# Attention of layer 0: scores in runs of nine over seven PSUM tiles of one bank, an exponential per bank, row sums of eight key blocks by DMA

## The chip, the core and the metric

The kernel runs on one core of a Trainium2 chip. TensorE (PE) multiplies, ScalarE (ACT) takes exponentials and copies, VectorE (DVE) adds and normalises, GpSimd (POOL) and SyncE (SP) issue DMAs, which all run on the core's 16 DMA engines. The metric is the device time of one execution in microseconds (us), the median over several executions. A profile is one execution recorded by the hardware profiler; its span can differ a little from the median.

## The reference, cut to what matters

Two images x of 256 channels and 64 x 64 pixels go through two layers. The change is in layer 0 alone, an attention over all 4096 pixels with eight heads of 32 channels:

```python
x = x + _L0_conv_ref(_gn(x), L0_conv_qkv_w, L0_conv_qkv_b, 8)

# _L0_conv_ref(x, qkv_w, qkv_b, num_heads), b = 2, c = 256, n = 4096
qkv = jnp.einsum('bchw,oc->bohw', x, qkv_w) + qkv_b[None, :, None, None]
qkv = qkv.reshape(b, 3, num_heads, head_dim, n)
q, k, v = (qkv[:, 0], qkv[:, 1], qkv[:, 2])
scale = 1.0 / math.sqrt(head_dim)
attn_logits = jnp.einsum('bhci,bhcj->bhij', q, k) * scale
attn_weights = jax.nn.softmax(attn_logits, axis=-1)
out = jnp.einsum('bhij,bhcj->bhci', attn_weights, v)
```

`_gn` normalises over groups of eight channels. Layer 1 is a block of convolutions and small local attentions. It comes after layer 0 of each image and is the same in both kernels.

## The kernel before

The two images (b = 0, 1) are worked through one after the other: statistics and projections, then `attention0`, then layer 1. The projections leave queries and keys in memory as two halves of 32-bit numbers whose sum is the exact value, so that a score is one matmul of fp32r operands with 128 rows (32 channels times four combinations of halves).

**Groups, blocks, units.** An image has 16 groups g: head g // 2 with one half of the 4096 queries, 2048 of them as four columns of T = 512. The keys come in NJ = 32 blocks j of 128. One unit is the score of one key block with one query column, a 128 x 512 matmul into one PSUM bank (L505), so a group has 128 units and an image 2048. ACT takes the exponential of a unit from PSUM (L511) and writes it to SBUF. Then two things are done with it:

- TensorE multiplies it with the values, `quarters` (L521). The four units of a block go to four partition quarters of the group's accumulator `av`, with 32 columns of weights each. A block counts as two steps of 256 columns each ("half blocks" below; each is four matmuls, which the trace shows as eight records), and blocks 0 and 31 are one step of 512 columns.
- its sum over the keys is prepared, `add_rows`: for most blocks DVE adds the unit to the tiles `e` (L550, L558), and for the blocks listed in SUMMED the DMA engines add it to the four parts of `acc` (`add_in_memory`, L566 for the first, a copy, and L568 for the accumulating ones). POOL issues these DMAs. They wait for the exponential and for the addition before them in the same rows. At the next group's start DVE adds `acc` to `e` (L748). Then TensorE sums over the partitions with a matrix of ones (`sum_rows`), ACT copies the product (L598), and some small DMAs and DVE instructions divide the group's result by it (`finish`).

**Places.** Exponentials live in a ring of RING = 28 places of 512 columns each, 17 in the tile `es` and 11 at the end of the tile `v`. In the profile their name is `es` or `v` accordingly. `places` holds the place of each unit, `n_places` counts places given out. A place is written again 28 places later, after the value product, the DVE addition or the DMA that reads it.

**PSUM.** Eight banks: `sa` of three, `sb` of two, `sc` of two, and `av` of one. `scores(spare)` fills all three tiles, seven units, with one exponential for each tile (or two where the ring wraps). When a statistic or a row sum needs a bank (`spare`), `sa` gets two units only and its third bank is lent out.

**The order.** It is written by hand, in a block under `manual_schedule`, for PE, ACT and DVE; the queues of POOL and SP follow their waits in program order. A loop alternates a run of scores with a stretch of value products. How many products go between two runs is worked out from `ready` (blocks whose scores stood before the latest run), `share` (an even spread of the steps, less two) and `must` (blocks whose places the next runs will write again). `wanted` is a queue of uses of a lent bank; one is done after two steps of a round, or at its end. A round ends at a group's end, so that the copy of `av` (L762) can go ahead before the next group's first product. `fetch_head` (at block 4 of an even group: keys and values of the next head) and `fetch_queries` (at a group's end, for the group after the next) issue SP's loads, which wait for free buffers.

The last group of an image is finished in another way: its last three blocks are summed by TensorE straight from the exponentials, in a bank lent at block NJ - 3.

Of the kernel before, what the change touches and what calls it, by code (L numbers as in the profile page):

```python
# [9 lines left out]
F32 = mybir.dt.float32  # L10
I32 = mybir.dt.int32
F32R = mybir.dt.float32r
AF = mybir.ActivationFunctionType
# [4 lines left out]
P = 128  # L18
B, C, H, W = 2, 256, 64, 64
N = H * W  # L20
T = 512
# [4 lines left out]
NH0 = C // HD0  # L26
# [14 lines left out]
def direct_layers(ctx: ExitStack, tc: tile.TileContext, a: dict, out: bass.AP, bad: bass.AP):  # L41
# [3 lines left out]
    nc = tc.nc  # L45
# [11 lines left out]
    psum = {}  # L57
# [307 lines left out]
    SC0 = 1.0 / math.sqrt(HD0)  # L365
# [8 lines left out]
    NJ = N // P  # L374
# [76 lines left out]

    RING, RING_A = 28, 17

    SUMMED = (3, 7, 11, 15, 18, 22, 26)

    def summed(g):

        return SUMMED if g else SUMMED[1:]

# [4 lines left out]
    def attention0(b, xts, held):  # L464
# [10 lines left out]
        n_units = NH0 * 2 * NJ * 4  # L475
# [4 lines left out]
        places = []  # L480
        n_places = 0

        def at_places(first, n):

            while n > 0:
                at = first % RING
                m = min(n, (RING_A if at < RING_A else RING) - at)
                yield m, es[:, at : at + m, :] if at < RING_A else held["es"][:, at - RING_A : at - RING_A + m, :]
                first, n = first + m, n - m

        def scores(spare):

            nonlocal n_places
            bank = None
            for tag, size in (("sa", 3), ("sb", 2), ("sc", 2)):
                first = len(places)
                n = min(size - (spare and size == 3), n_units - first)
                if n <= 0:
                    break
                sc = psum["sc"].tile([P, size, T], F32, tag=tag, name=f"{tag}_{b}_{first}")  # L500
                if spare and size == 3:
                    bank = sc[:, size - 1, :]
                for i in range(n):
                    g, (j, u) = (first + i) // (4 * NJ), divmod((first + i) % (4 * NJ), 4)
                    nc.tensor.matmul(  # L505
                        sc[:, i, :], held["k", g // 2][:, j * P : (j + 1) * P], held["q", g, u // 2][:, u % 2, :],
                        start=True, stop=True,
                    )
                i = 0
                for m, dst in at_places(n_places, n):  # L510
                    nc.scalar.activation(dst, sc[:, i : i + m, :], AF.Exp, scale=SC0)  # L511
                    i += m
                places.extend(range(n_places, n_places + n))
                n_places += size
            return bank

        def quarters(dst, lhs, rhs, start, stop, part=None):

# [17 lines left out]
        def add_rows(g, j):  # L536
            if j == 0:
                sums[g] = psum["sc"].tile([P, T], F32, tag="av", name=f"av_{b}_{g}")
                added[g] = [w4([P, 2, T], f"e_{b}_{g}_{w}") for w in range(2)]
                return  # L540
            for w in range(2):
                dst = added[g][w]
                if j in summed(g):
                    if w == 0:
                        add_in_memory(g, j)
                    continue
                if j == 1:
                    first = two_units(g, 0, w), two_units(g, 1, w)
                    if len(first[0]) == len(first[1]) == 1:
                        nc.vector.tensor_add(dst, first[0][0][1], first[1][0][1])  # L550
                    else:
                        for s in range(2):
                            nc.vector.tensor_add(dst[:, s, :], unit(g, 0, 2 * w + s), unit(g, 1, 2 * w + s))
                    continue
                for s, src in two_units(g, j, w):
                    if g == last and j in SUMMED_LAST:
                        continue
                    nc.vector.tensor_add(dst[:, s, :], dst[:, s, :], src)  # L558
# [11 lines left out]
        def work_of(g, j):  # L570


            if (g, j) < (last, NJ - 3):
                add_rows(g, j)
            for part in (None,) if j in (0, NJ - 1) else range(2):
                if part == 1:
                    yield
                quarters(
                    sums[g], held["v"][:, (g // 2) % 2, j, :], lambda u: unit(g, j, u), j == 0, j == NJ - 1, part
                )  # L580

        def sum_rows(g, rows):
            if g == last:
                for part in range(2):
                    for j in SUMMED_LAST:
                        quarters(rows, ones, lambda u: unit(g, j, u), j == SUMMED_LAST[0], False, part)
                    quarters(rows, ones, lambda u: acc[u], False, False, part)
                    quarters(rows, ones, lambda u: added[g][u // 2][:, u % 2, :], False, True, part)
                return
            quarters(rows, ones, lambda u: added[g][u // 2][:, u % 2, :], True, True)  # L590
# [140 lines left out]
        def steps():  # L731

            for done in range(NH0 * 2 * NJ):
                g, j = divmod(done, NJ)
                if (g, j) == (last, NJ - 3):
                    assert len(places) == n_units
                    held["rows"] = psum["sc"].tile([P, 3, T], F32, tag="sa", name=f"rows_{b}")[:, 2, :]
                    for i in (NJ - 3, NJ - 2, NJ - 1):
                        add_rows(g, i)
                    sum_rows(g, held["rows"])  # L740
                for _ in work_of(g, j):
                    yield done
                if g and j == 0:

                    for w in range(2):
                        dst = added[g - 1][w]
                        for s in range(2) if w == 0 else (slice(0, 2),):
                            nc.vector.tensor_add(dst[:, s, :], dst[:, s, :], acc[s] if w == 0 else pair)  # L748
                    waiting.clear()
                if g and j == 1:  # L750
                    wanted.append(late[0].send)
                if g and j in (9, 17):
                    next(late[0])
                for what in also.get((g, j), ()):
                    what()
                if j == 4 and g % 2 == 0 and g // 2 + 1 < NH0:
                    fetch_head(b, g // 2 + 1, held)
                if j == NJ - 1:
                    waiting.append(g)
                    avs = w4([P, 2, T], f"avs_{b}_{g}")  # L760
                    if g < last:
                        nc.scalar.copy(avs[:, 0, :], sums[g])  # L762
                    copied[g] = avs
                    late[:] = [finish(g)]
                    next(late[0])
                    if g + 2 < NH0 * 2:
                        fetch_queries(b, g + 2, held)
                yield done + 1

        E = mybir.EngineType  # L770
        with tc.manual_schedule(engines={E.PE, E.Activation, E.DVE}):

            per_group = 2 * NJ - 2
            work, begun, taken = steps(), 0, 0
            scores(False)
            final = False
            while not final:
                have = len(places)  # L780
                use = wanted.pop(0) if wanted else None
                bank = scores(use is not None)
                final = have == n_units
                ready = have // 4
                share = have * per_group // (4 * NJ) - 2

                must = sum(place < n_places + 7 - RING for place in places[: 4 * ready : 4])
                if must % NJ == 1:
                    must += 1
                assert must <= ready  # L790
                here = 0
                while begun < ready and (taken < share or begun < must or final or use is not None):
                    if use is not None and here == 2:
                        use(bank)
                        use = None
                        continue
                    here += 1
                    group = begun // NJ
                    begun = next(work)
                    taken += 1  # L800
                    if begun // NJ > group and begun >= must and not final and use is None:
                        break
                if use is not None:
                    use(bank)
            assert next(work, None) is None
            return *finish_last(last), st
# [585 lines left out]
    for b in range(B):  # L1392
        xts = x_first if b == 0 else ahead["xts"]
        w0 = w0_first if b == 0 else ahead["w0"]
        with tc.tile_pool(name=f"ps0_{b}", bufs=8, space=PSUM) as psum["ps"]:
# [7 lines left out]
            held = project0(b, xn, w0)  # L1403
# [571 lines left out]
```

## Time and profile before

| | us |
|---|---|
| median of 3 executions | 3120.94 (3116.66 to 3121.48) |
| span of the profiled execution | 3116.4 |
| attention of image 0 (118 to 1161 us of the span) | 1043 |
| attention of image 1 (1666 to 2709 us) | 1043 |
| ACT L511, exponentials of three banks (es and v) | 810 in 556 |
| ACT L511, exponentials of two banks | 1249 in 1214 |
| DVE L558, additions of 1024 columns | 1553 in 1332 |
| DVE L558, additions of 512 columns | 179 in 264 |

The span is the time from the first to the last instruction of the profiled execution. The four last rows add up the page's groups by shape. Busy times of different engines lie beside one another and don't add up to the span. A matmul's record lasts longer than the time to the next one's start[...]: distances from start to start tell what a matmul costs. The same holds for ACT, in smaller measure.

### The profile page before, as it was taken

The page shows a single profiled execution, that of the slowest core. Times are in us where ns is not written, and L with a number is a line of the kernel's source. Part 1 is how long each engine was busy: PE and PEld are TensorE (multiplying, and loading weights), DVE is VectorE, ACT ScalarE, POOL GpSimd, SP SyncE. Part 2 cuts the span into 40 slices and gives each one's busy share as a digit, 9 for nine tenths or more (in the row PEclk, how much of TensorE's full clock was granted, in tenths as well). Part 3 has the DMA queues.
Part 4 walks back from the last instruction along what each step waited for, and adds up shares of the span by engine and source line. Part 5 has one row for each costly group of instructions (what it writes and reads, how often), then busy time and mean ns, then how long its engine had stood idle before and what let it go on. Part 6 is the DMA issues. An engine that isn't in the chain of part 4 may idle for free. (4 is left out here: it accounts for less than half of the span.)

```text
span 3116.4 us, 62659 instructions
## 1 busy us (share of the span) xinstructions
PE 3031.2 (97%) x25129; PEld 1830.6 (59%) x25129; DVE 2467.0 (79%) x3126; ACT 2313.6 (74%) x2436; POOL 836.7 (27%) x923
## 2 busy tenths in 40 slices
PE   6999999999999999999989999999999999999998
PEld 4555555555555556677755555555555555476765
DVE  4599989999899999856556998989989999834543
ACT  2699999999999984622237999999999999734333
POOL 2022222222222231055301222222222222305440
PEclk9999999999999999999999999999999999999999
DMA  7969679797897761230159687796888975700000
GB/s 241 270 132 185 143 150 172 154 178 150 164 181 154 145 133 33 75 134 29 41 193 268 128 176 151 156 176 138 177 162 164 181 153 123 170 4 4 21 14 22
DMA packets 243787, 424.41 MB, mean 136 GB/s; under 512 B 99112, under 2 KB 109916, under 8 KB 241308
## 3 DMA queue, kind: packets, MB, share of 16 engines
q0 software_dynamic: 94992, 238.36, 39.8%
q1 hardware_dynamic: 147580, 181.68, 21.6%
q8 instruction: 199, 3.26, 0.4%
q14 instruction: 104, 0.85, 0.1%
q10 hardware_dynamic: 912, 0.27, 0.0%
HBM read 119.03 MB, written 68.39 MB: 60 GB/s over the span
## 5 line engine op out<-in xcount | busy, mean ns | idle before, releaser
L558 DVE TENSOR_TENSOR e<-e,es 128x1024 f32<-128x1024 f32 (+1 forms) x956 | 1038.6, 1142 | 79.6 <-ACT es L511 77.9
L521 PE MATMUL av<-es,v 128*32 128x256 f32 (+1 forms) x9644 | 746.7, 390 | 0.0
L558 DVE TENSOR_TENSOR e<-e,v 128x1024 f32<-128x1024 f32 (+1 forms) x640 | 675.2, 1107 | 47.7 <-ACT v L511 46.6
L511 ACT ACTIVATE es<-sa 128x1536 f32<-128x1536 f32 (+1 forms) x444 | 635.7, 1432 | 93.1 <-PE sa L505 54.9
L505 PE MATMUL sa<-q,k 128*128 128x512 f32 x1736 | 561.4, 430 | 9.2 <-ACT avs L598 3.5
L521 PE MATMUL av<-v 128*32 128x256 f32 (+1 forms) x6228 | 506.5, 389 | 0.0
L521 PEld LDWEIGHTS av<-es,v 128*32 128x32 f32 x9644 | 316.1, 109 | 299.4 <-issue 160.6
L505 PEld LDWEIGHTS sa<-q,k 128*128 128x128 f32 x1736 | 280.0, 188 | 291.8 <-issue 135.4
L505 PE MATMUL sc<-q,k 128*128 128x512 f32 x1180 | 371.4, 396 | 1.7 <-ACT es L511 0.7
L505 PE MATMUL sb<-q,k 128*128 128x512 f32 x1180 | 371.0, 395 | 1.1 <-ACT es L511 1.1
L521 PEld LDWEIGHTS av<-v 128*32 128x32 f32 x6228 | 216.5, 109 | 178.6 <-issue 81.2
L511 ACT ACTIVATE es<-sc 128x1024 f32<-128x1024 f32 x296 | 306.9, 1037 | 0.0
L511 ACT ACTIVATE v<-sc 128x1024 f32<-128x1024 f32 x294 | 304.9, 1037 | 0.1
L511 ACT ACTIVATE es<-sb 128x1024 f32<-128x1024 f32 x296 | 302.0, 1020 | 3.8 <-DMA acc<-es 3.8
L511 ACT ACTIVATE v<-sb 128x1024 f32<-128x1024 f32 x294 | 300.0, 1020 | 0.0
L505 PEld LDWEIGHTS sb<-q,k 128*128 128x128 f32 x1180 | 221.2, 188 | 55.4 <-ACT es L511 2.9
L505 PEld LDWEIGHTS sc<-q,k 128*128 128x128 f32 x1180 | 210.5, 188 | 71.8 <-ACT es L511 12.1
L511 ACT ACTIVATE v<-sa 128x1536 f32<-128x1536 f32 (+1 forms) x146 | 209.2, 1433 | 35.6 <-PE sa L505 17.0
L948 PE MATMUL mm<-v,wf 128*128 128x256 f32 x1024 | 227.6, 380 | 1.5 <-DVE z L957 1.5
L568 POOL DMA_DIRECT2D es<-es x116 | 98.9, 853 | 475.6 <-ACT es L511 424.3
L948 PEld LDWEIGHTS mm<-v,wf 128*128 128x128 f32 x1024 | 193.3, 190 | 36.8 <-issue 9.9
L938 POOL TENSOR_TENSOR v<-col 128x512 f32<-128x512 f32 x128 | 165.1, 1316 | 179.2 <-ACT rk_sr L1089 39.2
(262 smaller groups left out, 3179.0 us busy)
## 6 DMA issues: line engine op xcount, KB each, us to landing
acc<-es POOLq DMA_DIRECT2D x128, 512.0 KB, 6.2
acc<-v POOLq DMA_DIRECT2D x84, 512.0 KB, 6.4
es<-es POOLq DMA_DIRECT2D x136, 256.0 KB, 4.5
v<-es POOLq DMA_DIRECT2D x132, 256.0 KB, 5.1
k<-wk_halves SPq DMA_DIRECT2D x64, 512.0 KB
q<-wq_halves SPq DMA_DIRECT2D x256, 128.0 KB
v<-v POOLq DMA_DIRECT2D x90, 256.0 KB, 5.4
es<-v POOLq DMA_DIRECT2D x86, 256.0 KB, 3.9
```

Of the source, the lines that this page charges most:

```text
L505: nc.tensor.matmul(sc[:, i, :], held["k", g // 2][:, j * P : (j + 1) * P], held["q", g, u // 2][:, u % 2, :], start=True, stop=True,)
L511: nc.scalar.activation(dst, sc[:, i : i + m, :], AF.Exp, scale=SC0)
L521: nc.tensor.matmul(dst[HD0 * u : HD0 * u + HD0, n], lhs, rhs(u)[:, n], start=start, stop=stop)
L558: nc.vector.tensor_add(dst[:, s, :], dst[:, s, :], src)
L568: nc.gpsimd.dma_start(out=dst, in_=src, accum_op=ALU.add)
L938: (nc.gpsimd.tensor_add if plus else nc.gpsimd.tensor_sub)(dst, rows(one), rows(two))
L948: nc.tensor.matmul(mm[:, m, r, :], wf[:, k, 4 * r + q, m * P : (m + 1) * P], v[r // 2][:, r % 2, k, :], start=k == 0, stop=k == KC - 1,)
```

## The change

The three PSUM tiles become seven tiles of one bank, `s0` to `s6`, which `next_bank` gives out in turn together with a place. `scores` issues PHASE = 9 units, each with its own exponential. A lent bank is the next one in turn. SUMMED has eight blocks instead of seven, four or three apart in turn. The loop counts differently: it issues a run first and treats all but the last seven scores as `ready` (`behind`), `must` looks ten places ahead (`reach`), the last two steps of a group are done without regard to `share`, and the three last blocks of the image wait until all scores are issued.

```diff
--- before.py
+++ after.py
@@ -451,7 +451,7 @@

     RING, RING_A = 28, 17

-    SUMMED = (3, 7, 11, 15, 18, 22, 26)
+    SUMMED = (3, 6, 10, 13, 17, 20, 24, 27)

     def summed(g):

@@ -488,31 +488,27 @@
                 yield m, es[:, at : at + m, :] if at < RING_A else held["es"][:, at - RING_A : at - RING_A + m, :]
                 first, n = first + m, n - m

-        def scores(spare):
+        BANKS, PHASE = 7, 9
+
+        def next_bank():

             nonlocal n_places
-            bank = None
-            for tag, size in (("sa", 3), ("sb", 2), ("sc", 2)):
-                first = len(places)
-                n = min(size - (spare and size == 3), n_units - first)
-                if n <= 0:
-                    break
-                sc = psum["sc"].tile([P, size, T], F32, tag=tag, name=f"{tag}_{b}_{first}")
-                if spare and size == 3:
-                    bank = sc[:, size - 1, :]
-                for i in range(n):
-                    g, (j, u) = (first + i) // (4 * NJ), divmod((first + i) % (4 * NJ), 4)
-                    nc.tensor.matmul(
-                        sc[:, i, :], held["k", g // 2][:, j * P : (j + 1) * P], held["q", g, u // 2][:, u % 2, :],
-                        start=True, stop=True,
-                    )
-                i = 0
-                for m, dst in at_places(n_places, n):
-                    nc.scalar.activation(dst, sc[:, i : i + m, :], AF.Exp, scale=SC0)
-                    i += m
-                places.extend(range(n_places, n_places + n))
-                n_places += size
-            return bank
+            at = n_places
+            n_places += 1
+            return at, psum["sc"].tile([P, T], F32, tag=f"s{at % BANKS}", name=f"s_{b}_{at}")
+
+        def scores():
+
+            for unit in range(len(places), min(len(places) + PHASE, n_units)):
+                g, (j, u) = unit // (4 * NJ), divmod(unit % (4 * NJ), 4)
+                at, sc = next_bank()
+                nc.tensor.matmul(
+                    sc, held["k", g // 2][:, j * P : (j + 1) * P], held["q", g, u // 2][:, u % 2, :],
+                    start=True, stop=True,
+                )
+                ((_, dst),) = at_places(at, 1)
+                nc.scalar.activation(dst[:, 0, :], sc, AF.Exp, scale=SC0)
+                places.append(at)

         def quarters(dst, lhs, rhs, start, stop, part=None):

@@ -734,7 +730,7 @@
                 g, j = divmod(done, NJ)
                 if (g, j) == (last, NJ - 3):
                     assert len(places) == n_units
-                    held["rows"] = psum["sc"].tile([P, 3, T], F32, tag="sa", name=f"rows_{b}")[:, 2, :]
+                    held["rows"] = next_bank()[1]
                     for i in (NJ - 3, NJ - 2, NJ - 1):
                         add_rows(g, i)
                     sum_rows(g, held["rows"])
@@ -773,27 +769,32 @@


             per_group = 2 * NJ - 2
+            behind, reach = 7, PHASE + 1
             work, begun, taken = steps(), 0, 0
-            scores(False)
-            final = False
-            while not final:
-                have = len(places)
+            while begun < NH0 * 2 * NJ:
+                scores()
                 use = wanted.pop(0) if wanted else None
-                bank = scores(use is not None)
-                final = have == n_units
-                ready = have // 4
+                bank = next_bank()[1] if use is not None else None
+                final = len(places) == n_units
+                have = n_units if final else len(places) - behind
+                ready = max(0, have) // 4
                 share = have * per_group // (4 * NJ) - 2

-                must = sum(place < n_places + 7 - RING for place in places[: 4 * ready : 4])
+                must = sum(place < n_places + reach - RING for place in places[: 4 * ready : 4])
                 if must % NJ == 1:
                     must += 1
                 assert must <= ready
                 here = 0
-                while begun < ready and (taken < share or begun < must or final or use is not None):
+                while begun < ready:
                     if use is not None and here == 2:
                         use(bank)
                         use = None
                         continue
+                    ending = taken % per_group >= per_group - 2
+                    if not (taken < share or ending or begun < must or final or use is not None):
+                        break
+                    if not final and begun == NH0 * 2 * NJ - 3:
+                        break
                     here += 1
                     group = begun // NJ
                     begun = next(work)
```

## The prediction

> **What bounds the kernel now.** I read the busy table first, then the two stretches in which layer 0's attention runs, then a few microseconds of TensorE and ScalarE inside one, then the row-sum DMAs.
>
> ```profile
> PE 3031.2 (97%) x25129; PEld 1830.6 (59%) x25129; DVE 2467.0 (79%) x3126; ACT 2313.6 (74%) x2436; POOL 836.7 (27%) x923
> ...
> 118.00:1161.00 1043.00, 1037.92 (x10184) 590.86 (x10188) 955.56 (x978) 972.38 (x923) 276.27 (x339) 1.00 0.80 161
> 1666.00:2709.00 1043.00, 1037.51 (x10184) 590.18 (x10188) 955.71 (x978) 971.78 (x920) 272.70 (x338) 1.00 0.80 160
> 570.00:640.00 70.00, 69.73 (x691) 39.86 (x687) 66.98 (x68) 65.38 (x63) 17.16 (x21) 1.00 0.66 130
> 640.00:700.00 60.00, 60.00 (x594) 33.85 (x586) 53.68 (x54) 56.35 (x54) 17.19 (x21) 1.00 1.00 195
> ```
>
> The first line sums over the span. The others give start and end, length, then PE, PEld, DVE, ACT, POOL busy time, granted clock, DMA share, GB/s. The two stretches of 1043 us are the two batches' attention, 2086 of 3116 us, and the only part the change touches. There TensorE is never idle, DVE and ACT are busy 92 to 93% and the DMA engines 80%. The last two lines show how uneven the 80% is: one group of 128 scores with 0.66, the next with 1.00.
>
> ```profile
> 604.75 1.50 PE L521 MATMUL av<-es,v 128*32 128x256 f32 x24
> 606.18 0.96 PE L505 MATMUL sa<-q,k 128*128 128x512 f32 x3
> 606.98 0.63 PE L505 MATMUL sb<-q,k 128*128 128x512 f32 x2
> 607.45 0.63 PE L505 MATMUL sc<-q,k 128*128 128x512 f32 x2
> 608.00 1.50 PE L521 MATMUL av<-es,v 128*32 128x256 f32 x24
> 609.43 0.73 PE L505 MATMUL sa<-q,k 128*128 128x512 f32 x2
> ```
>
> This is one round of seven scores and three half blocks of value products (eight records each). A round lasts 609.43-606.18 = 3.25 us; with four half blocks 3.68, so a half block costs 0.43. Single records in this window start 0.2305 us apart among the scores, but 0.337 after a run's first, 0.327 from the last score to the first product, 0.24 after the first four products instead of 0.216, and 0.329 from the last products to the next score. Changing over and back thus costs 0.107+0.097+0.024+0.113 = 0.34 us a round, inside "busy" time.
>
> ```profile
> 605.32 1.02 ACT L511 ACTIVATE v<-sb 128x1024 f32<-128x1024 f32 x1
> 606.22 1.03 ACT L511 ACTIVATE v<-sc 128x1024 f32<-128x1024 f32 x1
> 607.18 1.46 ACT L511 ACTIVATE v<-sa 128x1536 f32<-128x1536 f32 x1
> 608.53 1.01 ACT L511 ACTIVATE v<-sb 128x1024 f32<-128x1024 f32 x1
> 609.43 1.03 ACT L511 ACTIVATE v<-sc 128x1024 f32<-128x1024 f32 x1
> ```
>
> An exponential lasts longer than the distance to the next: 0.90 us from start to start after two banks, 1.35 after three. Seven banks take 3.15 of the 3.25 us: ACT is second by little.
>
> ```profile
> acc<-es POOLq DMA_DIRECT2D x128, 512.0 KB, 6.2
> ...
> es<-es POOLq DMA_DIRECT2D x136, 256.0 KB, 4.5
> ...
>   POOL acc L568: 101.8, 49
>   ACT es L511: 5.6, 6
> ```
>
> The first two lines (queue, size, median us to landing) are the row-sum DMAs; the last two list who waited for the accumulator's tile: POOL 102 us, since one addition must land before the next goes into the same rows, and ACT 5.6 us.
>
> **What the skill says.** "TensorEngine Tiling (Array Packing)", Key Properties: "Changing tiling mode (not just tile) drains the TensorE". Scores use 128*128 tiles, products 128*32; the 0.34 us above agrees. "ScalarE: Activation LUTs", What ACT_TABLE_LOAD costs: an ACTIVATE with immediates takes 186 ns + 0.833 ns an element, and successive ones overlap by about 93 ns. The trace agrees on the duration (1039 ns for 1024 elements against 1.02 to 1.03 us) but shows more overlap, 0.11 to 0.13 us. "DMA: Bandwidth & Descriptors", Queues, rings and completion order: an engine alternates between queues that have work, packet by packet. That fits row-sum DMAs that land in 8.7 us at 685.88 while queries are loaded.
>
> **The change part by part.** Counted in the built instruction order, the attention has 588 score runs before and 454 after, with the same 4096 scores and 2128 half blocks.
>
> *Fewer changes of mode.* 134 x 0.34 = 45.6 us less on TensorE, the path that sets the end. The model (4096 x 0.2305 + 2128 x 0.432 + 588 x 0.34 = 2063) gives 99% of the 2086 us seen, so I trust its difference.
>
> *A separate bank for the row-sum product.* Before, it lies in the third bank of sa, and the next round's first score waits for its copy at L598: product to score takes 0.52 us instead of 0.33 at each group's end. After, that bank comes round seven tiles later. 30 x 0.19 = 5.7, taken as 5 us less.
>
> *Seven banks under nine scores.* Scores eight and nine need the banks of the run's first two. The first exponential can start 0.54 us after the run's first score (0.50 of matmul, 0.04 as seen at 607.18) and lasts about 0.6; the second ends by 1.65. Score nine starts at 0.337 + 7 x 0.2305 = 1.95, and its products need no later exponential (behind = 7). So no wait, with 0.3 us to spare: any later delay on ACT reaches TensorE at once.
>
> *4096 exponentials of one bank instead of 1770 larger ones.* Start to start is not shown for this form. Nearest rows: 1347/3 = 449 ns per bank, and the 128x512 copies L762 and L1017, followed after 462 to 465 ns; the skill's price gives 612-93 = 519. I take 465. A round on ACT is 9 x 0.465 = 4.19; on TensorE 9 x 0.2305 + 0.34 + 0.43 a half block, 4.14 with four, 4.57 with five. The commonest pattern is four, four, five: 12.85 against 12.56. ACT stays behind TensorE by 2%; ragged rounds cost, I estimate, 5 us (0 to 30).
>
> *An eighth summed block.* DVE gets 54 additions of 1.216 us and 20 of 0.683 fewer: 79 us. It was hidden: joining each addition with the exponential that next overwrites its source, the smallest distance is 3.8 us, the median 10. Worth nothing. POOL issues 796 DMAs instead of 676; 120 x about 0.95 = 114 us of issue time on a queue 27% busy, nothing by itself. But the engines get 254/222 = 1.14 times the row-sum traffic, in less time.
>
> The same join for DMAs: a block of scores must have landed in its sum about 12.3 us after its exponentials, when the ring of 28 places comes round. In groups that don't load a head it lands after 6 to 9, leaving 3 to 6. In the 14 that load the next head's keys and values, blocks 7 and 11 land after 10 to 13.5, leaving 0.1 to 2.6, and block 22, beside a load of queries, leaves 0.1 to 2.7. In those groups, away from loads, a block three after the last lands about 0.9 us later relative to its exponentials than its forerunner, a block four after 1.9 earlier. The new list goes 3, 4, 3, 4 ...: backlog no longer melts by 1.9 a step but by 1 a pair. Banks one by one loosen the limit by about 0.8 us (a place need not wait for two neighbours). Block 6 now meets the load head on; blocks 10, 13 and 20 or 24 then arrive 0.3 to 1.5 late. Sum about 2 us a group, less the 0.3 to spare: 1.7 x 14 = 24 us. Ends: 0 if the looser limit suffices, 5.2 x 14 = 73 if each step loses another 0.7 (the service of 7.5 us per block seen from 664 to 695, against the new 6.74 of distance).
>
> *Moved with it.* The merge after a group now waits for block 27 instead of 26, some 2 us later; additions queue behind it on DVE, whose 10 us hide that, and the row-sum product comes about four blocks later. Loads on SP keep their steps. The start (runs of 14, now 18, behind a table load) and the end count as 0, within 2.
>
> Sum: -45.6 - 5 + 5 + 24 = -22 us. The profiled span of 3116.4 becomes 3095; the runs' median is 4.5 above the span, so 3099.
>
> **The rivals.** *All hidden (0.18).* For: odd groups have 3 to 6 us to spare, and the ring's limit loosens. Against: 0.1 left in many even groups. -51 +0 to 5: 3072.
> *The ring waits (0.20), the slower side.* ACT stands before a place that a row-sum DMA still reads, in each of 14 head-loading groups. For: a share of 1.00 in 640 to 700 already. Against: spare room in the gap around a group's start. -51+5+73 = +27: 3148. It decides from 46/14 = 3.3 us a group.
> *ACT becomes the bound (0.10).* At 519 ns, 128 x 0.519 + 0.92 for two copies is 67.4 us a group against 63.6 on TensorE: +121-51 = +70, 3191. Slower from 502 ns. Against: every row of 512 elements without pointers is followed within 465.
> *Both balance (0.10)*: 3121. That includes that the runs don't shorten TensorE, should the change-over grow with nine scores; nothing shows that.
>
> **How the numbers follow.** The forecast has 0.42, its own range 3076 to 3114. Faster: 0.42+0.18 = 0.60; within 0.2% (6 us, about what a measurement can tell) 0.10; slower 0.20+0.10. The range runs from all hidden less 6, 3066, to past the ring rival, 3155; the ACT rival and a rest are outside.
>
> **What would show it.** TensorE rounds of 4.14 and 4.57 us confirm the first step; no product-to-score distance of 0.52 the second. Exponentials start to start at 465 confirm the third; 500 or more makes ACT the bound. ACT's waits for landing DMAs, 5.6 us before, should be near 30, in even groups; near 80 means slower, near 5 all hidden. A merge that holds up the row-sum product on TensorE would be a step I left out.

## The result, and the profile after

The changed kernel takes 3120.8 us (median of 12 runs, 3115.25 to 3124.48), the kernel before on the same chip 3117.85 us (12 runs). The ratio is 1.001 with a 95% interval of 1.0002 to 1.0018, some 3 us more: no change that matters. The forecast of 22 us less did not come. The profiled spans are 3118.1 and 3116.4 us.

First the busy table and the four stretches that the prediction showed, now of the changed kernel (the columns are the same):

```profile
PE 3035.6 (97%) x25129; PEld 1867.0 (60%) x25129; DVE 2389.4 (77%) x3052; ACT 2419.6 (78%) x4762; POOL 941.6 (30%) x1043
...
118.00:1161.00 1043.00, 1039.32 (x10135) 607.25 (x10137) 915.54 (x939) 1025.71 (x2086) 328.86 (x398) 1.00 0.89 178
1666.00:2709.00 1043.00, 1039.88 (x10152) 608.53 (x10154) 917.14 (x943) 1026.92 (x2086) 324.82 (x398) 1.00 0.89 178
570.00:640.00 70.00, 70.00 (x686) 41.34 (x678) 64.94 (x67) 69.48 (x143) 22.32 (x27) 1.00 0.82 159
640.00:700.00 60.00, 60.00 (x596) 35.20 (x599) 50.71 (x54) 59.95 (x123) 18.86 (x23) 1.00 1.04 204
```

In an attention of 1043 us ACT was busy for 972 us and is now for 1026: from 640 to 700 it has 0.05 us left. DVE has 40 us less per image, POOL 53 more, the DMA share went from 0.80 to 0.89. All of this was forecast in kind; ACT's size was not. TensorE looks as busy as before, but a score's record (413 ns in the mean) is longer than the 230 ns or so to the next one's start, so a short wait leaves no idle time. Next the groups of the changed kernel's page (busy time, mean ns of one; then idle time just before, and what ended most of it):

```profile
L510 ACT ACTIVATE es<-s 128x512 f32<-128x512 f32 x2500 | 1263.4, 727 | 12.2 <-PE s L505 7.3
...
L505 PEld LDWEIGHTS s<-q,k 128*128 128x128 f32 x4096 | 732.8, 188 | 440.1 <-ACT es L510 192.7
...
L510 ACT ACTIVATE v<-s 128x512 f32<-128x512 f32 x1596 | 823.2, 736 | 7.4 <-PE s L505 5.5
```

The exponentials hardly wait (12.2 + 7.4 us in the whole span). The weight loads' idle time has to be read with care: the first load of every run of scores has 0.41 us of it, in the kernel before as well (median 0.412 in both), where TensorE goes from products to scores, and the list puts this down to the exponential that ended last, if one ended just then. Of the 312 us that the scores' loads wait for exponentials (192.7 for those into `es`, 119.8 for those into `v`), only 115 lie inside runs. Before, these were 25 of 130. Now the timeline of ACT (start, duration, count) in the stretch with the busiest DMA engines:

```profile
654.99 8.62 ACT L510 ACTIVATE es<-s 128x512 f32<-128x512 f32 x17
663.37 5.63 ACT L510 ACTIVATE v<-s 128x512 f32<-128x512 f32 x11
668.61 8.71 ACT L510 ACTIVATE es<-s 128x512 f32<-128x512 f32 x17
677.05 5.66 ACT L510 ACTIVATE v<-s 128x512 f32<-128x512 f32 x11
682.30 8.74 ACT L510 ACTIVATE es<-s 128x512 f32<-128x512 f32 x17
```

Start plus duration is where a row ends: 663.61, 669.00, 677.32, 682.71, 691.04. From end to end that is 5.39 us for 11 exponentials, 8.32 for 17, 5.39 and 8.33: **0.490 us for each**. From start to start the rows give less (5.24 us for 11 between 663.37 and 668.61, 0.476 each), because an exponential's record begins ever earlier before its predecessor's end, which also stretches the mean duration to 727 ns. So ends, not starts, tell what an exponential costs; that starts tell it too, as was said ahead of the prediction, doesn't hold here. Over both images 3998 of the 4030 distances between successive ends are 0.48 to 0.50 us; 32 are longer than 0.52, by 16 us together.

What this does to TensorE is seen in the starts of its runs of nine scores:

```profile
607.74 2.33 PE L505 MATMUL s<-q,k 128*128 128x512 f32 x9
611.86 2.47 PE L505 MATMUL s<-q,k 128*128 128x512 f32 x9
616.12 2.62 PE L505 MATMUL s<-q,k 128*128 128x512 f32 x9
620.97 2.35 PE L505 MATMUL s<-q,k 128*128 128x512 f32 x9
625.11 2.45 PE L505 MATMUL s<-q,k 128*128 128x512 f32 x9
629.35 2.62 PE L505 MATMUL s<-q,k 128*128 128x512 f32 x9
634.20 0.97 PE L505 MATMUL s<-q,k 128*128 128x512 f32 x3
```

Rounds of four, four and five half blocks take 4.12, 4.26 and 4.85 us, in sum 13.23 (607.74 to 620.97, and again to 634.20). The forecast's TensorE time was 12.85; 27 exponentials at 0.490 are 13.23. The runs themselves grow from 2.33 to 2.62 us: scores eight and nine stand before a bank whose exponential is late (the ninth starts 0.288 us after the eighth in the mean, where 0.247 is seen when exponentials are cheap, in narrow_exp below). ACT sets the pace.

Last, who waited for the tile `acc` of the row sums:

```profile
  POOL acc L564: 39.5, 12
  POOL es L562: 8.3, 1
  ACT es L510: 4.7, 7
  ACT v L510: 1.8, 3
```

ACT waited 6.5 us for landing row-sum DMAs (5.6 before). The median landing time of a 512 KB addition is 6.2 us as before. Yet POOL's wait for the addition before fell from 101.8 to 39.5 us: there is one more block to add and less waiting.

### The profile page after: what moved, and what is told of

Its sections match the earlier page's. It is cut to its first block, busy times and chain, and to the rows that moved or that the text cites. A ratio compares the mean times of both kernels' runs of the same rounds, so it can differ in the third digit from the quotient of the medians.

```text
span 3118.1 us, 65880 instructions
## 1 busy us (share of the span) xinstructions
PE 3035.6 (97%) x25129; PEld 1867.0 (60%) x25129; DVE 2389.4 (77%) x3052; ACT 2419.6 (78%) x4762; POOL 941.6 (30%) x1043
## 5 line engine op out<-in xcount | busy, mean ns | idle before, releaser
L510 ACT ACTIVATE es<-s 128x512 f32<-128x512 f32 x2500 | 1263.4, 727 | 12.2 <-PE s L505 7.3
L505 PE MATMUL s<-q,k 128*128 128x512 f32 x4096 | 1130.0, 413 | 6.3 <-ACT es L510 2.6
L554 DVE TENSOR_TENSOR e<-e,es 128x1024 f32<-128x1024 f32 (+1 forms) x910 | 990.3, 1147 | 86.1 <-ACT es L510 85.7
L505 PEld LDWEIGHTS s<-q,k 128*128 128x128 f32 x4096 | 732.8, 188 | 440.1 <-ACT es L510 192.7
L510 ACT ACTIVATE v<-s 128x512 f32<-128x512 f32 x1596 | 823.2, 736 | 7.4 <-PE s L505 5.5
L564 POOL DMA_DIRECT2D acc<-es x156 | 153.6, 993 | 178.7 <-ACT v L510 84.0
L564 POOL DMA_DIRECT2D v<-es x134 | 140.7, 1050 | 46.7 <-ACT es L510 26.9
L564 POOL DMA_DIRECT2D es<-v x86 | 74.5, 866 | 260.4 <-ACT v L510 212.8
L564 POOL DMA_DIRECT2D acc<-v x96 | 96.3, 1003 | 103.7 <-ACT es L510 62.0
L562 POOL DMA_DIRECT2D es<-v x14 | 7.9, 567 | 371.6 <-ACT v L510 317.5
L564 POOL DMA_DIRECT2D v<-v x88 | 91.3, 1037 | 30.9 <-ACT es L510 18.7
```

Source lines behind the costliest of these rows:

```text
L505: nc.tensor.matmul(sc, held["k", g // 2][:, j * P : (j + 1) * P], held["q", g, u // 2][:, u % 2, :], start=True, stop=True,)
L510: nc.scalar.activation(dst[:, 0, :], sc, AF.Exp, scale=SC0)
L564: nc.gpsimd.dma_start(out=dst, in_=src, accum_op=ALU.add)
```

## The experiments

Theory A, after the first look: ACT is the bound, at 0.49 us per exponential, and what was saved on TensorE and what was added on the DMA engines are both hidden behind it. Theory B: the row-sum DMAs ate the gain. Theory C: runs of nine over seven banks don't shorten TensorE's work at all. All medians, with the ratio to the kernel before on the same chip (95% interval); distances to the kernel before are given below by this ratio, of 3117 us:

| kernel | us | ratio |
|---|---|---|
| after_seven | 3118.94 | 1.0008 (1.0000 to 1.0017) |
| before_eight | 3133.86 | 1.0054 (1.0041 to 1.0067) |
| narrow_exp | 3071.49 | 0.9852 (0.9839 to 0.9865) |
| narrow480 | 3083.32 | 0.9893 (0.9878 to 0.9908) |
| narrow_seven | 3063.30 | 0.9822 (0.9809 to 0.9836) |
| rows_on_dve | 3117.73 | 1.0009 (1.0000 to 1.0017) |
| copies_on_dve | 3116.27 | 1.0002 (0.9994 to 1.0010) |
| before_single | 3186.20 | 1.0220 (1.0206 to 1.0233) |
| tiles2221 | 3159.21 | 1.0132 (1.0117 to 1.0148) |
| tiles_9_8 | 3134.12 | 1.0065 (1.0052 to 1.0078) |
| tiles2221_runs7 | 3119.73 | 1.0003 (0.9994 to 1.0012) |
| after_runs7 | 3110.35 | 0.9980 (0.9973 to 0.9986) |
| after_runs8 | 3110.62 | 0.9976 (0.9967 to 0.9985) |
| runs7_seven | 3101.50 | 0.9947 (0.9934 to 0.9960) |
| runs8_seven | 3101.62 | 0.9948 (0.9935 to 0.9962) |

**The eighth summed block, alone and undone.** before_eight gives the kernel before the new list; after_seven gives the changed kernel the old one:

```diff
-    SUMMED = (3, 7, 11, 15, 18, 22, 26)
+    SUMMED = (3, 6, 10, 13, 17, 20, 24, 27)
```

> The kernel before with the new list of eight summed blocks and nothing else. A: within 4 us of the kernel before: TensorE is the bound there, and DMAs and DVE are hidden. B: 20 us or more slower. C: within 4 us.

> The changed kernel with the old list of seven summed blocks. A (ACT is the bound: an exponential of one bank retires every 490 ns whatever else happens): within 4 us of the changed kernel, so about 3 us above the kernel before, although row-sum traffic falls by an eighth. B (row-sum DMAs hold up the ring of places): 20 us or more faster than the changed kernel. C (TensorE pays by itself in runs of nine): as the changed kernel.

The eighth block costs the kernel before 17 us. Who waited for its `acc`:

```profile
  POOL acc L568: 196.2, 85
  ACT es L511: 13.0, 12
  ACT v L511: 2.8, 5
```

POOL's wait for the addition before went from 101.8 to 196.2 us, and ACT's for DMAs from 5.6 to 15.8. All three theories had this kernel wrong: A and C expected under 4 us, B 20 or more. In the changed kernel the same list makes no difference that can be told: 1.0010 with eight, 1.0008 with seven, each within 0.0009. So the row-sum DMAs did not eat the gain there: theory B falls.

**Cheaper exponentials.** narrow_exp and narrow480 leave out a quarter and a sixteenth of each exponential's columns, once each place was written in full (those columns keep older values); all else is the changed kernel.

```diff
-                nc.scalar.activation(dst[:, 0, :], sc, AF.Exp, scale=SC0)
+                w = 3 * T // 4 if at % RING in written else T
+                written.add(at % RING)
+                nc.scalar.activation(dst[:, 0, :w], sc[:, :w], AF.Exp, scale=SC0)
```

> The changed kernel with exponentials of 384 of the 512 columns, once each place has been written in full; the other quarter of the exponentials is left out. All matmuls, additions and DMAs stay. A: one retires every 0.43 x 0.75 + 0.06 = 0.38 us, TensorE is the bound again and the whole forecast gain appears: 40 to 51 us below the kernel before. B: within 5 us of the changed kernel, since the DMAs are the same. C: within 5 us of the changed kernel, since TensorE's work is the same.

narrow_exp ends 46 us below the kernel before. Its TensorE rounds and ACT's waits:

```profile
600.27 2.33 PE L506 MATMUL s<-q,k 128*128 128x512 f32 x9
604.40 2.33 PE L506 MATMUL s<-q,k 128*128 128x512 f32 x9
608.96 2.34 PE L506 MATMUL s<-q,k 128*128 128x512 f32 x9
613.09 2.33 PE L506 MATMUL s<-q,k 128*128 128x512 f32 x9
```

```profile
ACT es L513 <- PE s L506: 176.3, 242, 1.8
...
ACT v L513 <- PE s L506: 116.9, 154, 1.8
...
ACT es L513 <- DMA acc<-es: 17.5, 15, 2.4
...
ACT v L513 <- DMA acc<-v: 13.9, 9, 2.4
```

Rounds last 4.13 and 4.56 us, as the model has them (4.14, 4.57), every run 2.33. An exponential of 384 columns ends 0.383 us after the one before. ACT now waits 293 us for scores. Theory C falls: the runs of nine do save what was worked out. From its first score to the first product after it, a run of nine takes 2.32 us in the mean here and 2.41 in the changed kernel: over 450 runs 44 us, nearly all that lies between the two. And with TensorE in front, the row-sum DMAs show: ACT waits 31.4 us for them.

narrow_seven takes narrow_exp's exponentials with the old list of seven blocks, and narrow480 asks whether the price alone explains the miss:

```diff
-                w = 3 * T // 4 if at % RING in written else T
+                w = 15 * T // 16 if at % RING in written else T
```

> The changed kernel with exponentials of 384 columns (a quarter left out, as in narrow_exp) and the seven summed blocks of the kernel before. ScalarE is then far from the bound, so the row-sum DMAs' own cost under runs of nine shows: if the term of 24 us for them is real and only hidden behind ScalarE in the full kernel, this one ends 10 to 25 us below narrow_exp, and ScalarE's waits for landing DMAs fall from 31 us to under 12. If the term is not real under runs of nine, it is within 4 us of narrow_exp.

> The changed kernel with exponentials of 480 of the 512 columns once each place was written in full: it leaves out one sixteenth of those exponentials' columns. By the ends of successive exponentials (0.428 us per bank and 0.06 of its own) each one then takes 0.428 x 480/512 + 0.06 = 0.461 us, close to the 0.465 that the forecast's sum used. If the price of an exponential was the only wrong term of that sum, this kernel ends 15 to 35 us below the kernel before (the forecast had 22). If near-equal totals of ScalarE and TensorE also cost, because long rounds at a group's change leave ScalarE idle and seven banks can't carry that over, it ends only 0 to 15 us below, with ScalarE still busy over 92% of the attention and waiting in the changes of group.

```profile
ACT v L513 <- DMA acc<-v: 7.5, 7, 1.9
...
ACT es L513 <- DMA acc<-es: 0.8, 2, 0.4
```

In narrow_seven (its waits above) ACT waits 8.3 us for row-sum DMAs, 23 less. The time falls by 9 us against narrow_exp by the ratios, by 11 by the spans, at or just below the lower end expected: the DMA term is real under runs of nine, but it is about 10, not 24.

narrow480's exponentials end 0.4625 us apart (16 of them from 614.72 to 622.12 in this timeline):

```profile
601.29 8.01 ACT L513 ACTIVATE es<-s 128x480 f32<-128x480 f32 x17
609.51 5.21 ACT L513 ACTIVATE v<-s 128x480 f32<-128x480 f32 x11 [0.20 <-PE s L506]
614.56 7.56 ACT L513 ACTIVATE es<-s 128x480 f32<-128x480 f32 x16
```

That is nearly the price that the forecast took, and the kernel is 33 us faster than before (29 to 38 by the interval), inside what "price alone" expected. Here ACT waits for a score now and then (the 0.20; 49 us in all). So 0.03 us of an exponential, six per cent, decide over 36 us. From there on a cheaper exponential brings little: 0.08 us less in narrow_exp, 13 us.

**Relief for ACT by moving its copies.** rows_on_dve gives the copy of the row sums to DVE, copies_on_dve that of `av` as well:

```diff
-            nc.scalar.copy(avs[:, 1, :], rows)
+            nc.vector.tensor_copy(avs[:, 1, :], rows)
...
-                        nc.scalar.copy(avs[:, 0, :], sums[g])
+                        nc.vector.tensor_copy(avs[:, 0, :], sums[g])
```

> The changed kernel with the copy of a group's row sums on DVE instead of ACT (30 copies). A: ACT loses 30 x 0.48 us of copies, and up to 0.4 us more after each of them: 12 to 26 us below the changed kernel. C or row-sum DMAs as the bound: within 3 us of the changed kernel. If DVE gets to the copy late, the bank comes back late and part of it is lost.

> The changed kernel with both copies of a group, row sums and value products, on DVE. A: ACT loses 60 x 0.49 us and what follows the first kind: 27 to 40 us below the changed kernel, unless the next group's first product waits for DVE, which may be some us behind: then up to 30 x 2 us slower than that.

Neither can be told from the changed kernel, though 12 to 26 and 27 to 40 us were expected. ACT's waits in copies_on_dve:

```profile
ACT es L510 <- PE s L505: 22.7, 34, 2.9
ACT v L510 <- PE s L505: 19.0, 26, 1.7
```

These were 7.3 and 5.5: ACT's busy time per image fell from 1026 to 1013 us, and its wait for scores rose by 29 in the two images. A copy happens at a group's change, where TensorE has its longest rounds (six to eight half blocks, or four or five and the row-sum product) and ACT runs out of scores. Time freed at that place becomes idle time. It is the steady rounds that lack ACT.

**Exponentials of two banks under runs of eight and nine.** tiles2221 makes the seven banks tiles of 2, 2, 2 and 1, with an exponential per tile and runs of five tiles; tiles_9_8 has tiles a, b, c of one bank and x, y of two, in runs of nine and eight scores; tiles2221_runs7 is the first with runs of four tiles:

```diff
-        BANKS, PHASE = 7, 9
+        SIZES, RUN, PHASE = (2, 2, 2, 1), 5, 9
...
+            return at, most, psum["sc"].tile([P, most, T], F32, tag=f"s{tag}", name=f"s_{b}_{at}")
...
+                for m, dst in at_places(at, n):
+                    nc.scalar.activation(dst, sc[:, i : i + m, :], AF.Exp, scale=SC0)
```

```diff
+        TAGS, ENDS = "abxycab" + "cxyabc", (7, 0)
...
+            most = 2 if tag in "xy" else 1
...
+                if n_tiles % len(TAGS) in ENDS:
+                    break
```

```diff
-        SIZES, RUN, PHASE = (2, 2, 2, 1), 5, 9
+        SIZES, RUN, PHASE = (2, 2, 2, 1), 4, 7
```

> The changed kernel with four PSUM tiles of two, two, two and one banks, an exponential per tile, and runs of five tiles (nine or eight scores). A: ACT has 1614 x 0.915 + 868 x 0.490 = 1902 us of exponentials instead of 2007, TensorE is the bound with 468 runs; 40 us less, given back in part because the fifth tile of a run waits for the exponential of its first tile (two banks, done about 0.1 us late, some 350 times): 5 to 45 us below the kernel before. B: as the changed kernel. C: as the changed kernel or slower.

> The changed kernel with seven banks as three tiles of one (a, b, c) and two of two (x, y), runs of nine (abxyc ab) and eight (cxyab c) in turn, an exponential per tile. The tiles that a run takes a second time are single ones, done in time. A: ACT has 2296 x 0.49 + 900 x 0.915 = 1949 us of exponentials, 58 less than the changed kernel; TensorE with 484 runs is the bound, 104 x 0.34 = 35 us below the kernel before, of which row-sum DMAs may take back 5 to 15: 20 to 35 us below the kernel before. If run-internal waits persist as with tiles of two, two, two and one: no gain.

> The changed kernel with tiles of two, two, two and one banks, an exponential per tile, and runs of four tiles (seven scores), so that no run takes a tile twice. A: ACT has 1901 us of exponentials instead of 2007 and is off the path; TensorE with 584 runs sets the pace, as in the kernel before, but no bank is missing from a round: 5 to 20 us below the kernel before. If the wait inside a run was not what cost with runs of nine: 30 us or more above it.

None gains anything, though theory A had all three below the kernel before. tiles2221 is 41 us slower than before. Its TensorE:

```profile
310.97 2.60 PE L518 MATMUL s<-q,k 128*128 128x512 f32 x9
315.37 2.58 PE L518 MATMUL s<-q,k 128*128 128x512 f32 x9
320.17 2.58 PE L518 MATMUL s<-q,k 128*128 128x512 f32 x9
```

A run of nine takes 2.6 us instead of 2.33 and its round 4.40 instead of 4.14: the fifth tile, scores eight and nine, is the first one again and waits for the end of a two-bank exponential, which holds both banks (the eighth score starts 0.392 us after the seventh in the mean, in the changed kernel 0.244). That stops TensorE inside its run, while ACT waits 84 us for scores in this kernel: neither engine is full. In tiles_9_8, 20 us slower, the weight loads of the row-sum products wait about 1 us for the exponential of their lent bank at a group's change, 29 times. In tiles2221_runs7 ACT is relieved (987 us busy per image), but it waits 61 us for scores and 19.8 for row-sum DMAs, and the kernel ends level with the one before; that the DMAs are what takes its gain was not tried.

**An exponential per bank alone.** before_single splits the exponentials of the kernel before, whose tiles stay of three and two banks:

```diff
-                for m, dst in at_places(n_places, n):
-                    nc.scalar.activation(dst, sc[:, i : i + m, :], AF.Exp, scale=SC0)
-                    i += m
+                for i in range(n):
+                    ((_, dst),) = at_places(n_places + i, 1)
+                    nc.scalar.activation(dst[:, 0, :], sc[:, i, :], AF.Exp, scale=SC0)
```

> The kernel before with one exponential per bank (4096) from its tiles of three, two and two banks, all else as it is: the part of the change that burdens ACT, alone. A: ACT needs 128 x 0.49 + 0.98 = 63.7 us a group beside TensorE's 64.8, and cannot bank what it gains in long rounds for short ones: 5 to 25 us above the kernel before. If ACT's price of an exponential doesn't matter: within 3 us.

It costs 69 us, far more than expected. Inside its runs the weight loads of `sc` wait for exponentials, and ACT in turn waits for the first scores of the next run:

```profile
PEld sc L505 <- ACT es L511: 67.3, 175, 0.7
PEld sc L505 <- ACT v L511: 65.5, 176, 0.7
```

```profile
L511 ACT ACTIVATE es<-sa 128x512 f32<-128x512 f32 x1306 | 716.8, 670 | 54.9 <-PE sa L505 45.5
```

The waits of `sc` were 12.1 and 6.0 before. This tile of two banks comes free only after its second exponential, the last of a run, so a run's sixth score waits for all exponentials of the run before. Scores six and seven start 0.294 us after their forerunners in the mean, before 0.238 and 0.233. That makes 0.115 us a run of seven and 63 us in all 552 of them, nearly the whole loss. ACT has idle time in its turn: 197 of the distances between the ends of its exponentials are over 0.52 us, by 64 us together (32 and 16 us in the changed kernel). With tiles of one bank the sixth score would need the sixth exponential alone. runs7_seven, below, has as many exponentials, runs of seven and seven blocks too, but tiles of one bank, and is 85 us faster than this kernel; it also counts its products the new way and lends banks from outside the run, and these were not tried apart from the tiles.

**The length of the runs.** With ACT as the bound, shorter runs should do no harm. after_runs7 and after_runs8 set the run to 7 and 8 scores in the changed kernel; runs7_seven and runs8_seven also take the old list of seven blocks:

```diff
-        BANKS, PHASE = 7, 9
+        BANKS, PHASE = 7, 8
```

> The changed kernel with runs of seven scores instead of nine (584 instead of 454), all else as it is. A (ACT is the bound at 490 ns an exponential): TensorE gets 130 x 0.34 = 44 us more, but ACT hides most of it, so 0 to 20 us above the changed kernel. C (the runs of nine are what costs): at or below the changed kernel, since that cost is gone. TensorE as the bound in the changed kernel: 44 us above it.

> The changed kernel with runs of eight scores (510 instead of 454). A, refined (between a group's 32nd and last unit ACT sets the pace at 0.49 us a unit whatever the run length, only the first 32 units follow TensorE): within 8 us of the kernel before, as the changed kernel and the one with runs of seven. TensorE as the bound: 19 us above the changed kernel.

> The changed kernel with runs of seven and the old list of seven summed blocks. A: within 5 us of the same with eight blocks (7 us below the kernel before); row-sum DMAs cost 0.27 us in each of 14 head-loading groups there, so up to 4 us less. If DVE needs the eighth block: slower.

> The changed kernel with runs of eight scores over the seven banks and the seven summed blocks. If ScalarE's pace of 0.49 us per bank sets the time in both, it lies within 6 us of runs of seven with seven blocks (3101), the runs of eight saving changes of mode that are hidden. If changes of mode still decide, it is 8 to 15 us faster than that. If eight scores over seven banks hold TensorE up, it is 6 us or more slower.

Both lengths are faster than before, by 6 and 7 us, and by 16 or 17 with seven blocks: the fastest kernels that leave nothing out. Theory A had runs of seven 0 to 20 us above the changed kernel; they are about 10 below it. So with ACT in front, runs of nine do cost something. In the changed kernel ACT waits 12.8 us for scores, in after_runs7 5.4. Nine scores over seven banks bind the two engines more closely; that this is the reason is argued, not shown. ACT in runs8_seven, by its groups and its waits:

```profile
L510 ACT ACTIVATE es<-s 128x512 f32<-128x512 f32 x2498 | 1293.9, 933 | 0.5 <-PE s L505 0.4
```

```profile
ACT avs L758 <- PE av L517: 10.5, 30, 0.4
...
ACT v L510 <- DMA acc<-v: 0.5, 1, 0.5
ACT es L510 <- PE s L505: 0.4, 1, 0.4
ACT v L510 <- PE s L505: 0.4, 2, 0.2
```

Nothing holds its exponentials up. Its attention of 1034.4 and 1032.6 us per image (first score to start of the last product) is ACT's floor for this order: 2048 x 0.490 is 1003.5, 32 copies with their waits take 21.4 from end to end, and 6.4 pass from the last exponential to the last product, in sum 1031; the rest are the start and 1 us of other waits. Runs of seven and eight come out alike (3101.50, 3101.62), though runs of seven change mode more often: that saving is hidden now. The changed kernel stands 19 us above this floor in two images. Its ACT waits 12.8 us for scores and 6.5 for DMAs, about that distance. In after_runs8 the waits for scores are 2.4, in after_seven those for DMAs 1.1: the first alone brings 10 us, the second none that can be told, both together the 19.

Where the 16 us come from, although ACT has more to do than before, is seen in the mean time of a group of 128 scores (groups 1 to 14 of both images), with the first 32 scores, where the group before is finished, apart:

| kernel | group | first 32 | other 96 |
|---|---|---|---|
| before | 64.77 | 17.91 | 46.89 |
| after | 64.70 | 17.35 | 47.34 |
| narrow_exp | 63.26 | 16.88 | 46.39 |
| runs7_seven | 64.26 | 17.39 | 46.86 |

runs7_seven gains all its 0.5 us at the change of group, where the kernel before lends the third bank of `sa` and shortens a run; waits for the copy of a row sum, found below, are 4.3 us of the 16, and the rest was not tried apart. The changed kernel gains as much there and gives it back in the steady rounds, whose 96 exponentials take 47.04 at 0.490.

## Why the prediction was wrong

**The mis-sized term: "I take 465".** The step was "4096 exponentials of one bank instead of 1770 larger ones", priced at 465 ns each; it measured 490. The prediction read distances from start to start (0.90 us after two banks, 1.35 after three), and copies followed after 462 to 465. The same lines, read at their ends, have 606.34, 607.25, 608.64, 609.54, 610.46. Over all of the trace of before, ends are 0.915 us apart for two banks (median), and 1.343 for three in the dozen that follow their predecessor closest (the others start late, for want of scores). That makes 0.428 for a bank and 0.06 for the instruction: 0.49 for one bank was to be had beforehand. 4096 of them are 2007 us, against 1214 x 0.915 + 556 x 1.343 = 1858. The estimate from the Trainium skill ("ScalarE: Activation LUTs", What ACT_TABLE_LOAD costs: 612 less an overlap of 93 ns) was 519, too high by 29 where 465 was too low by 25; the measurement decides. The sign that the prediction named, starts 465 or 500 apart, would not have told the cases apart either: in the changed kernel starts are 477 apart (median) and ends 490.

**What hung on it.** The price set "ACT stays behind TensorE by 2%", and this turned: 13.23 us for the commonest three rounds against 12.85. "So no wait, with 0.3 us to spare" turned with it: the runs shown take 2.33 us in narrow_exp and up to 2.62 in the changed kernel. The +5 for ragged rounds became about 49, the distance from narrow_exp to the changed kernel. Of these, 30 lie between narrow_exp and runs8_seven, where ACT hardly stops, and the other 19 are about what ACT waits for scores and DMAs in the changed kernel.

The prediction's own working for the rivals, "slower from 502 ns", misses the second part: with 490 it gives 128 x 0.490 + 0.92 = 63.6 us a group, level with its 63.6 on TensorE, and so nearly the whole gain. Measured are 63.26 in narrow_exp, 64.20 in runs8_seven and 64.70 in the changed kernel. The rival "both balance" had the right idea for one half, and 0.10; its other half, that the runs don't shorten TensorE, is refuted by narrow_exp. That its 3121 is the time that came is luck: it is the old time, as the median of three runs, 3 us above that of all twelve.

**"Fewer changes of mode", -45.6: right.** narrow_seven, without ACT's limit and without the eighth block, is 55 us below before (51 to 60), against -51 for this and the row-sum bank together. narrow_exp's rounds match the model to 0.01 us.

**"A separate bank for the row-sum product", -5: right in size, read at the wrong place.** The distance of 0.52 us is no wait. It follows a group's last step, whose products have 512 columns and last longer than those of a half block, and it is there at all 30 changes of group in the changed kernel and in narrow_exp too. The row-sum product itself is always followed by value products. But the wait exists in the kernel before:

```profile
PEld sa L505 <- ACT avs L598: 16.7, 30, 0.8
```

The list puts 30 waits of first loads down to the copy L598. Less 0.41 us each for the change from products to scores, 4.3 us are left: in 12 of the 30 changes a run's first score starts 0.65 to 0.71 us after the last product instead of 0.31. Four more runs start 0.26 us late behind statistics in the lent bank, 5.4 us in all. In the changed kernel no run waits so.

**The row-sum DMAs, +24: real, too large, and hidden.** 17 us in the kernel before, about 10 with runs of nine, under cheap exponentials, 9 to 10 with runs of seven or eight (after_runs7 against runs7_seven) and none that can be told in the changed kernel. ACT's waits for DMAs in narrow_exp, 31.4 us, are near the 30 that the prediction named, yet cost only about 10. A wait for a DMA that ACT's own lateness covers costs nothing, so the two terms can't be added.

**The sum.** At nearly its own price, in narrow480, the sum of -22 would have come within its range: measured were -33. That is in part luck, since two errors offset: the DMAs were put too high by about 14, and the ragged rounds, which the 13 us from narrow_exp to narrow480 stand for, too low by about 8. That DVE's relief is worth nothing, that POOL's issues cost nothing and that the merge comes later without harm was not contradicted.

## What to carry to other kernels

Price an instruction of a saturated engine by the distance between the ends of successive ones, and get the fixed part from two sizes in the trace before a change makes them smaller: here 25 ns in 465 cost the whole gain. When two engines come within a few per cent of one another, a saving on one is worth what the other leaves, so try the cut on each alone; and the place counts, since relief at a group's change, where the other engine is late, brought nothing. And a list of waits can hold time that is no wait: compare it with distances from start to start, and with the same list of another kernel. An exponential per bank without tiles of one bank lost 69 us.

## What the hardware showed that was not expected

- A record's duration on ACT grows with the queue: exponentials of one bank have a mean duration of 727 ns in the changed kernel and 933 in runs8_seven, while their ends are 0.490 us apart in both. The duration holds waiting behind the predecessor; 4096 x 0.933 would be longer than the span.
- End to end, exponentials from PSUM took 0.383 us for 384 columns, 0.463 for 480, 0.490 for 512, 0.915 for 1024 and 1.343 for 1536 (medians; the last from the closest dozen): a straight line of 0.428 per 512 columns with about 0.06 of fixed cost.
- The chain of row-sum DMAs ran with far fewer waits behind exponentials of one bank. With seven blocks POOL waited for the addition before 101.8 us in the kernel before, but 8.0 in before_single and 4.3 in after_seven; with eight, 196.2 in before_eight and 39.5 in the changed kernel. A group takes 64.8 us in before and in after_seven alike, so it is not a slower pace. With exponentials of two banks (tiles2221_runs7) it is 132.5 at eight blocks, and 90.5 in narrow_exp, where exponentials are of one bank but ACT often waits for scores. So an even stream of exponentials may be it, which no run tried by itself.
